# Half of each row normalisation given to GpSimd, the residual added in PSUM for three chunks only, and routing and stores reordered around it

## The chip, the core and the metric

The kernel runs on one core of one Trainium2 chip, in float32 throughout. The metric is the device time of one launch in microseconds (us). The engines named below are PE (TensorE: matmuls, with PEld for its weight loads), DVE (VectorE), ACT (ScalarE), POOL (GpSimd, which also issues the indirect DMAs) and SP (SyncE, which issues nearly all other DMAs). Each engine executes its own instructions in the order in which the program issued them, and waits on semaphores for the others.

## The reference

One transformer block with adaptive layer norm (4096 tokens of width D = 256): linear attention, and then a mixture of 8 experts of which each token uses two.

```python
def layernorm(x): return (x - mean(x)) / sqrt(var(x) + 1e-5)

sa, ca, ga, sb, cb, gb = six rows of (silu(c) @ wmod)          # ga, gb kept off zero by 0.25
h = layernorm(x) * (1 + ca) + sa
x = x + ga * attention(h)                                      # 16 heads of 64, linear attention
h = layernorm(x) * (1 + cb) + sb
p = softmax(h @ Wg + bg); top 2 of 8 experts, weights renormalised
expert_e(h) = gelu(h @ W1[e] + b1[e]) @ W2[e] + b2[e]          # 256 -> 1024 -> 256
x = x + gb * sum over the two chosen experts of weight * expert_e(h)
```

## The kernel before, in words

**Attention (0 to about 344 us).** The 4096 tokens lie in 8 chunks `xs[0..7]` of 512 tokens (128 partitions x 4 tiles x 256). `hT[i]` is the first norm's output of chunk i, transposed. All of the linear attention folds into one 256 x 256 matrix; with 8 more columns for the experts' logits it is `weff`. `raw` holds what x itself gives to the logits.

**Residual and routing (about 344 to 415 us).** `products(i)` makes chunk i of the new x and its logits: `residual(i, half, cols)` takes, for each of 4 tiles of 128 tokens, the product `hT[i]` x `weff` (two blocks of K) and then adds `xs[i]` and `raw` in the same PSUM bank by multiplying with the identity matrix. A PSUM buffer `po` holds half a chunk; there are three. `park(i)` has ACT copy both halves to `xs[i]` and `logits` (`keep`) and has SP store `xs[i]` to the output (`store`).

A `Route` then ranks the tokens of its chunks: chunks 0, 1 and 2 alone, 3 and 4 together (`r34`), and 5, 6, 7 together (`last`). Its steps, in the order in which the data needs them:

- DVE: `chunk_stats` (mean and variance of each tile), `variance`; ACT: `root` (a square root, with a table load before and after it); DVE: `finish`, `distances` (logits less their maximum), `choose` (two largest, tile `both`).
- PE: `places`, matmuls of `both` with triangular and all-one matrices into PSUM tile `pp`: each token's running number within its expert. It includes `seen`, the count of all chunks before, so that the routes are a chain.
- DVE: `weigh` (weights into `row`), `aim` (reads `pp`, makes `dest` and the new `seen`).
- ACT: `rows`, the second norm of x, tile by tile, into `row`; POOL: `begin_rows` (token numbers into `row`) and `send`: for each tile two indirect DMAs that scatter the rows to `routed` in DRAM, sorted by expert.

After three chunks `early_table` counts how many full blocks of 256 rows the experts have and fills `where` for the first 5 blocks (`EARLY`), which hold rows of chunks 0 to 2 (`FIRST`) alone. `late_table` does it for the rest.

**Expert blocks (about 415 us to the end).** `run` takes the blocks one after the other: SP loads a block's weights (`load_weights`) and rows (`load_rows`, tile `xg`), three blocks ahead; `prepare` transposes the rows (PSUM tile `ptb`, copied by ACT to `xT`); `hidden` is 32 matmul instructions into `ph` and 8 gelus on ACT (`gl`); `project` is 32 or so into `py`; `add_to_out` adds the result to the output by indirect DMAs on POOL. `steps` hangs the remaining routing of chunks 5 to 7 between the first two blocks: `places` of `last` stands on PE behind block 0's `hidden` and block 1's `prepare`, and in front of block 1's `hidden`.

**Order.** From the residual part on, every call goes through `InOrder`, so the program text is the order of each engine's queue. In the loop over chunks 0 to 2 the text is: statistics and norm of chunk i, `park(i + 1)`, `rows`, `choose`, `places`, then `products(i + 2)`, `weigh`, `aim`, `send`. Behind the loop come `early_table`, the routing of `r34` up to `power`, `products` and `park` of 5, 6 and 7 with the `rows` of `r34`, and then `load_rows(0)` and the ranks of `r34`. On SP `load_rows(0)` stands behind the stores of all eight chunks.

Of the kernel before, what the change touches and what calls it, by code (L numbers as in the profile page):

```python
# [14 lines left out]
AF = mybir.ActivationFunctionType  # L15
ALU = mybir.AluOpType
# [6 lines left out]
TPC = 4  # L23
# [25 lines left out]
def adaln_block_kernel(  # L49
# [18 lines left out]
    on = SimpleNamespace(pe=nc.tensor, dve=dve, act=nc.scalar, pool=nc.gpsimd, sp=nc.sync)  # L68
    _, N, D = x.shape
    INNER = HEADS * DH  # L70
    E, _, H = w1.shape
    KB = D // P
# [3 lines left out]
    NCH = N // CH  # L76
# [9 lines left out]
    FIRST = 3  # L86
# [22 lines left out]
    ident = const.tile([P, P], FP, tag="ident", name="ident")  # L109
# [8 lines left out]
    xs = [const.tile([P, TPC, D], FP, tag=f"x{i}", name=f"x{i}") for i in range(NCH)]  # L118
    hT = [const.tile([P, KB, CH], FP, tag=f"hT{i}", name=f"hT{i}") for i in range(NCH)]
    mv = const.tile([P, NT, 2], FP, tag="mv", name="mv")  # L120
    rstd = const.tile([P, NT], FP, tag="rstd", name="rstd")
# [8 lines left out]
    raw = const.tile([P, NT, E], FP, tag="raw", name="raw")  # L130
# [62 lines left out]
    with tc.tile_pool(name="attn", bufs=1) as attn, tc.tile_pool(  # L193
# [58 lines left out]
        for half in range(2):  # L252
            cols = slice(half * 512, (half + 1) * 512)
# [32 lines left out]
        with tc.tile_pool(name="ps_t", bufs=4, space=bass.MemoryType.PSUM) as ps_t:  # L286
# [141 lines left out]
            for i in range(NCH):  # L428
                if i + 1 < NCH:
                    xn = first_norm(i + 1)  # L430
                for t in range(TPC):
                    n = i * TPC + t
# [42 lines left out]
        with tc.tile_pool(name="ps_c", bufs=1, space=bass.MemoryType.PSUM) as ps_c:  # L475
# [10 lines left out]
            for acc in pctx:  # L486
                nc.tensor.matmul(
                    acc, zeros[:, 0, :], zeros[:, :, :HW].to_broadcast([1, PPB, HW]),
                    start=True, stop=False,
# [69 lines left out]
            for s in range(NT + LAG):  # L559
# [6 lines left out]
                if s >= LAG:  # L566
                    add_context(s - LAG)
                    after_context(s - LAG)
                    i, rest = divmod(order[s - LAG], 3)
# [6 lines left out]
            for g, pairs in enumerate(groups):  # L576
                nq, q0 = len(pairs), pairs[0]
                nc.vector.reciprocal(zr[:, q0 : q0 + nq, :], pctx[g][:, :nq, DH:HW])
                for hh in range(2):
                    r = slice(hh * DH, (hh + 1) * DH)  # L580
# [17 lines left out]
            for kb in range(KB):  # L598
                pw = ps_w.tile([P, D], FP, tag="w", name="pw")
                for q in range(PAIRS):  # L600
# [4 lines left out]
                        start=(q == 0),  # L605
                        stop=(q == PAIRS - 1),
# [33 lines left out]
    logits = table.tile([P, NT, E], FP, tag="logits", name="logits")  # L640

    def residual(i: int, half: int, cols: int):

        po = ps_r.tile([P, 2, 512], FP, tag="r", name="po")
        for z in range(2):
            t = 2 * half + z
            for kb in range(KB):
                on.pe.matmul(
                    po[:, z, :cols],
                    hT[i][:, kb, t * P : (t + 1) * P],  # L650
                    weff[:, kb, :cols],
                    start=(kb == 0),
                    stop=False,
                )
            on.pe.matmul(po[:, z, :D], ident, xs[i][:, t, :], start=False, stop=(cols == D))
            if cols > D:
                on.pe.matmul(
                    po[:, z, D:cols], ident, raw[:, i * TPC + t, :], start=False, stop=True
                )
        return po  # L660

    def attention_logits():
# [34 lines left out]
    def stats_of(n: int, src):  # L697
        st = small.tile([P, 6], FP, tag="st", name="st")
        on.dve.bn_stats(st, src)
        on.dve.bn_aggr(mv[:, n, :], st)  # L700

    def chunk_stats(i: int):
        for t in range(TPC):
            stats_of(i * TPC + t, xs[i][:, t, :])

    def keep(i: int, half: int, po, more: bool = True):

        on.act.activation(xs[i][:, 2 * half : 2 * half + 2, :], po[:, :, :D], AF.Identity)
        if more:
            n = i * TPC + 2 * half  # L710
            on.act.activation(logits[:, n : n + 2, :], po[:, :, D : D + E], AF.Identity)
# [3 lines left out]
    def products(i: int):  # L715
        parts[i] = [residual(i, half, D + E) for half in range(2)]

    def park(i: int):
        for half, po in enumerate(parts.pop(i)):
            keep(i, half, po)  # L720
        store(i)

    class Norm:

# [42 lines left out]
    shift = table.tile([P, NT], FP, tag="shift", name="shift")  # L767

    def store(i: int):
        on.sp.dma_start(ov[i], xs[i])  # L770
# [6 lines left out]
    class Route:  # L777
# [28 lines left out]

        def rows(self, c: int = 0):

            for t in range(TPC):
                n = self.n0 + c * TPC + t  # L810
                on.act.activation(
                    self.row[c][:, t, :D], xs[self.chunks[c]][:, t, :], AF.Identity,
                    bias=shift[:, n : n + 1], scale=rstd[:, n : n + 1],
                )

        def distances(self, src=None):
# [78 lines left out]
            on.dve.tensor_reduce(here, self.both.rearrange("p t e -> p e t"), AX.X, ALU.add)  # L895
            on.dve.tensor_tensor(seen[:, 0, :], seen[:, 0, :], here, ALU.add)

        def send(self, *which):

            for t in [c * TPC + t for c in which for t in range(TPC)]:  # L900
                for k in range(2):
                    ins = on.pool.indirect_dma_start(
                        lists[(self.n0 + t) * 2 + k],
                        IndirectOffsetOnAxis(ap=self.dest[:, k, t : t + 1], axis=0),
                        self.row[t // TPC][:, t % TPC, :],
                        None,
                    )
                    if self.chunks[0] >= FIRST:
                        apart(ins, later_sends, early_loads)
# [117 lines left out]
    def tiles_of(b: int):  # L1027
        return BT if b < EARLY + PAIRED else 1
# [7 lines left out]
    def load_rows(b: int):  # L1036
        nt = tiles_of(b)
        first = register(0, b, E * N - nt * P)
        xg = xpool.tile([P, BT, ROW], FP, tag="xg", name="xg")
        ins = on.sp.dma_start(  # L1040
            xg[:, :nt, :], routed[ds(first, nt * P), :].rearrange("(j p) w -> p j w", p=P)
        )
        if b < EARLY:
            apart(ins, early_loads, later_sends)
        return xg
# [137 lines left out]
    def table_for(func):  # L1183

        on.act.activation(spare[:, 1:], spare[:, :1], func)
# [8 lines left out]
    for half in range(2):  # L1194
        po = residual(0, half, D)
# [2 lines left out]
        for z in range(2):  # L1198
            stats_of(2 * half + z, po[:, z, :D])
        keep(0, half, po, more=False)  # L1200
    store(0)
    pl = first_logits()
    products(1)
    for i, (r, norm) in enumerate(zip(routes[:FIRST], norms)):
        if i > 0:
            chunk_stats(i)
        norm.variance()
        norm.root()
        table_for(AF.Exp)
        norm.finish()  # L1210
        r.distances(pl if i == 0 else None)
        r.begin_rows()
        r.power()
        park(i + 1)
        r.rows()
        r.choose()
        r.places()
        products(i + 2)
        r.weigh()
        r.aim()  # L1220
        r.send(0)
    early_table()
    r34, norm = routes[3], norms[3]
    park(4)
    chunk_stats(3)
    products(5)
    chunk_stats(4)
    norm.variance()
    norm.root()
    table_for(AF.Exp)  # L1230
    norm.finish()
    r34.distances()
    r34.begin_rows()
    r34.power()
    weights = load_weights(0, None)
    for i in range(5, NCH):
        park(i)
        if i + 1 < NCH:
            products(i + 1)
        if i > 5:  # L1240
            r34.rows(i - 6)
    loads = {0: (load_rows(0), *weights[1:])}
    r34.choose()
    r34.places()
    r34.weigh()
    r34.aim()
    r34.send(0, 1)
    last = routes[4]
    for i in last.chunks:
        chunk_stats(i)  # L1250
    norms[4].iterate()
    last.distances()
    last.choose()
    residual_psum.close()
# [4 lines left out]

    steps = {  # L1260
        (0, 1): [last.power, last.begin_rows, lambda: last.rows(0), lambda: last.rows(1), last.places],
        (0, 2): [last.weigh, last.aim, lambda: last.send(0, 1)],
        (1, 1): [lambda: last.rows(2), lambda: last.send(2)],
        (1, 2): [late_table],
    }

    pairs, order_of = list(range(EARLY + PAIRED)), []
# [88 lines left out]
```

## Time and profile before

| | |
|---|---|
| median of 8 runs | 926.48 us (923.61 to 930.95) |
| profiled execution | 926.64 us; span of its instructions 924.9 us; mean granted PE clock 0.972 |
| busy in the span | PE 880.5, DVE 370.1, ACT 349.4, POOL 356.9 us |
| residual and routing | from 344.5 us (first `po`) to 415.1 us (first `ph`) |
| block 1's `hidden` starts | 428.96 us |
| first and last scatter of rows by POOL | 362.35 and 463.14 us |

In the lines of the profile a line number is that of the kernel; L36 is the helper of `InOrder`, through which most calls go, so the tiles' names tell the instructions apart. A float32 matmul appears as two instructions. "[3.03 <-PE pp L36]" means that the engine sat idle for 3.03 us before the instruction, and that what ended the wait was PE's write of `pp`. PEclk is the clock granted to PE, 1.00 being full speed.

### The profile page before, as it was taken

How to read it: one execution, taken by the hardware profiler on the slowest of the kernel's cores; microseconds unless marked ns; L12 is line 12 of the kernel's file. 1: busy time of each engine (PE TensorE's matmuls, PEld its weight loads, DVE VectorE, ACT ScalarE, POOL GpSimd, SP SyncE). 2: the span in 40 equal slices, each digit the busy share in tenths (PEclk: the TensorE clock that was granted, in tenths of full speed). 3: DMA queues.
4: the chain of work that ended last, by engine and by line, in shares of the span. 5: the costliest groups of instructions: out<-in, count | busy, mean ns of one | idle time of the engine just before them, and what ended most of it. 6: DMA issues, size and time to landing. Idle time of an engine off the chain costs nothing. (4 is left out here: it accounts for less than half of the span.)

```text
span 924.9 us, 13061 instructions
## 1 busy us (share of the span) xinstructions
PE 880.5 (95%) x4706; PEld 665.2 (72%) x4706; DVE 370.1 (40%) x915; ACT 349.4 (38%) x642; POOL 356.9 (39%) x311
## 2 busy tenths in 40 slices
PE   7979999999999889979999999999999999999993
PEld 4544444455545578868888888888989889898883
DVE  5454453798888846545611212112112111111111
ACT  4313443344434425347233233332443333334230
POOL 2000000377998912717733333233223233232423
PEclk9978999999999979989999999999999999999997
DMA  9999950133000002469887787775897777766511
GB/s 328 354 344 351 351 168 1 45 115 114 3 1 1 1 1 95 159 215 383 296 263 191 205 261 223 229 243 178 286 346 222 243 238 247 246 214 209 153 29 30
DMA packets 124535, 175.25 MB, mean 189 GB/s; under 512 B 12428, under 2 KB 105266, under 8 KB 124468
## 3 DMA queue, kind: packets, MB, share of 16 engines
q1 hardware_dynamic: 113040, 152.78, 50.2%
q0 software_dynamic: 11424, 21.61, 8.9%
q8 instruction: 38, 0.62, 0.3%
q14 instruction: 29, 0.24, 0.1%
q10 hardware_dynamic: 4, 0.00, 0.0%
HBM read 117.69 MB, written 57.71 MB: 190 GB/s over the span
## 5 line engine op out<-in xcount | busy, mean ns | idle before, releaser
L1107 ACT ACTIVATE gl<-ph,b_sb 128x256 f32<-128x256 f32 (+1 forms) x280 | 122.2, 437 | 258.8 <-PE ph L1100 252.2
L1118 PE MATMUL py<-w_sb,gl 128*128 128x256 f32 x960 | 212.7, 379 | 0.0
L1100 PE MATMUL ph<-xT,w_sb 128*128 128x256 f32 (+1 forms) x1120 | 208.0, 344 | 1.3 <-ACT xT L1074 1.3
L1100 PEld LDWEIGHTS ph<-xT,w_sb 128*128 128x128 f32 x1120 | 184.5, 191 | 21.4 <-ACT xT L1074 2.0
L1118 PEld LDWEIGHTS py<-w_sb,gl 128*128 128x128 f32 x960 | 180.0, 190 | 23.1
L1126 DVE SCALAR_TENSOR_TENSOR y<-py,gs,gb_bc 128x256 f32<-128x256 f32 x60 | 29.0, 484 | 310.5 <-PE py L1118 306.7
L277 PE MATMUL pq<-wq,hT 128*128 128x512 f32 x256 | 118.3, 604 | 1.2 <-DVE qs L36 1.2
L277 PE MATMUL pk<-wk,hT 128*128 128x512 f32 x256 | 117.0, 610 | 0.3 <-ACT hT L178 0.3
L36 POOL DMA_INDIRECT hT<-out_dram,who x35 | 36.9, 1055 | 158.5 <-DMA out_dram<-hT,who 149.7
L277 PEld LDWEIGHTS pk<-wk,hT 128*128 128x128 f32 x256 | 48.5, 195 | 60.6 <-issue 55.6
L36 POOL DMA_INDIRECT routed<-row,dest_i x64 | 62.6, 978 | 56.1 <-ACT row L36 19.5
L277 PEld LDWEIGHTS pq<-wq,hT 128*128 128x128 f32 x256 | 46.0, 190 | 49.5 <-issue 45.9
L36 POOL DMA_INDIRECT out_dram<-y,who x33 | 52.4, 1587 | 54.3 <-DVE y L1127 25.1
L36 POOL TENSOR_TENSOR qs<-qs,qsum 128x1024 f32<-128x1024 f32 x30 | 58.1, 1937 | 15.6 <-DVE qsum L36 15.6
L36 DVE TENSOR_TENSOR qs<-qs,pk 128x1024 f32<-128x1024 f32 x31 | 37.8, 1221 | 63.5 <-ACT ka L438 45.3
L36 POOL TENSOR_TENSOR hT<-hT,y 128x256 f32<-128x256 f32 x35 | 25.2, 720 | 79.6 <-DMA hT<-out_dram,who 54.4
L36 ACT ACTIVATE qs<-qs 128x1024 f32<-128x1024 f32 x32 | 33.8, 1055 | 38.2 <-DVE qs L36 38.2
L438 ACT ACTIVATE ka<-pk 128x1024 f32<-128x1024 f32 x24 | 24.6, 1023 | 57.6 <-PE pk L277 57.6
L483 POOL MEMSET qs<- 128x8 f32 x8 | 0.8, 116 | 113.5 <-PE pt L175 82.3
L36 DVE TENSOR_REDUCE qmax<-pq 128x16 f32<-128x1024 f32 x32 | 38.6, 1206 | 13.9 <-PE pq L277 13.8
L36 POOL TENSOR_TENSOR ka<-ka,nk_bc 128x1024 f32<-128x1024 f32 x18 | 42.5, 2359 | 0.0
L539 PEld LDWEIGHTS pctx<-qs,ka 128*64 128x64 f32 x768 | 26.0, 145 | 20.7 <-issue 12.6
(256 smaller groups left out, 1006.6 us busy)
## 6 DMA issues: line engine op xcount, KB each, us to landing
w_sb<-in_L_ffn_W_dram SPq DMA_DIRECT2D x80, 1024.0 KB, 6.0
routed<-pad SPq DMA_DIRECT2D x32, 1088.0 KB, 12.9
x<-in_L_attn_x_dram SPq DMA_DIRECT2D x16, 512.0 KB, 3.9
xg<-routed SPq DMA_DIRECT2D x28, 272.0 KB, 4.6
b_sb<-b_d SPq DMA_DIRECT2D x40, 128.0 KB, 5.4
out_dram<-x SPq DMA_DIRECT2D x8, 512.0 KB, 2.7
xg<-routed SPq DMA_DIRECT2D x12, 136.0 KB, 4.4
ka<-in_L_wmod_dram SPq DMA_DIRECT2D x3, 512.0 KB, 11.8
```

Source lines behind the costliest of these rows:

```text
L36: ins = getattr(self.engine, name)(*args, **kwargs)
L277: nc.tensor.matmul(pw[:, half * 512 : (half + 1) * 512], hT[i][:, kb, t * P : (t + 1) * P], w[:, kb, half * 512 : (half + 1) * 512], start ...
L438: nc.scalar.activation(k_tile(n), pk, AF.Identity)
L483: nc.gpsimd.memset(qs[:, :, (h + 1) * HW - 1 : (h + 1) * HW], 1.0)
L539: nc.tensor.matmul(pctx[g][h * DH : (h + 1) * DH, j, :], ek[:, q * P + h * DH : q * P + (h + 1) * DH], qs[:, q, h * HW : (h + 1) * HW], st ...
L1100: on.pe.matmul(ph[:, :rows], w1_sb[:, kb, hb * P : (hb + 1) * P], xT[:, kb, :rows], start=(kb == 0), stop=(kb == KB - 1),)
L1107: on.act.activation(gl[:, hb, :rows], ph[:, :rows], AF.Gelu_apprx_tanh, bias=b1_sb[:, hb : hb + 1])
L1118: on.pe.matmul(py, gl[:, hb, j * P : (j + 1) * P], w2_sb[:, hb, :], start=(hb == 0), stop=(hb == HB - 1),)
L1126: on.dve.scalar_tensor_tensor(y, py, gs[:, j : j + 1], gb_bc, ALU.mult, ALU.mult)
```

## The change

1. For chunks 3 to 7 `residual` no longer adds `xs[i]` and `raw` in PSUM. `keep` copies the product to `hT[i]` (`parked`), and DVE adds it to `xs[i]` (`add`, one instruction over 128 x 1024, followed by the chunk's statistics) and `raw` to the logits (`add_logits`).
2. `rows` on ACT does two of a chunk's four tiles; POOL does the other two (`other_rows`) ahead of the chunk's sends. `send` takes one chunk.
3. In the loop over chunks 0 to 2, `products(2)` and `products(3)` stand before `places`; `products(4)` stands behind `early_table`. The ranks and sends of `r34` stand before `products(6)`, no longer behind `products(7)`.
4. The stores: 0 to 2 behind their chunk's sends; 3 and 4 in block 2's step, 5 to 7 in block 3's. On SP `load_rows(0)` then stands behind the stores of chunks 0 to 2 alone.

```diff
     def residual(i: int, half: int, cols: int):
         po = ps_r.tile([P, 2, 512], FP, tag="r", name="po")
+        whole = i < FIRST
         for z in range(2):
             t = 2 * half + z
             for kb in range(KB):
...
-                    stop=False,
-                )
-            on.pe.matmul(po[:, z, :D], ident, xs[i][:, t, :], start=False, stop=(cols == D))
-            if cols > D:
-                on.pe.matmul(
-                    po[:, z, D:cols], ident, raw[:, i * TPC + t, :], start=False, stop=True
-                )
+                    stop=(kb == KB - 1 and not whole),
+                )
+            if whole:
+                on.pe.matmul(po[:, z, :D], ident, xs[i][:, t, :], start=False, stop=(cols == D))
+                if cols > D:
+                    on.pe.matmul(
+                        po[:, z, D:cols], ident, raw[:, i * TPC + t, :], start=False, stop=True
+                    )
         return po
+    def parked(i: int):
+        return xs[i] if i < FIRST else hT[i].rearrange("p kb (z d) -> p (kb z) d", d=D)
     def keep(i: int, half: int, po, more: bool = True):
-        on.act.activation(xs[i][:, 2 * half : 2 * half + 2, :], po[:, :, :D], AF.Identity)
+        on.act.activation(parked(i)[:, 2 * half : 2 * half + 2, :], po[:, :, :D], AF.Identity)
...
     def park(i: int):
         for half, po in enumerate(parts.pop(i)):
             keep(i, half, po)
-        store(i)
+
+    def add(i: int):
+        on.dve.tensor_tensor(xs[i], xs[i], parked(i), ALU.add)
+        chunk_stats(i)
+
+    def add_logits(*chunks):
+        tiles = slice(chunks[0] * TPC, (chunks[-1] + 1) * TPC)
+        on.dve.tensor_tensor(logits[:, tiles, :], logits[:, tiles, :], raw[:, tiles, :], ALU.add)
         def rows(self, c: int = 0):
-            for t in range(TPC):
+            for t in range(TPC // 2):
...
+        def other_rows(self, c: int):
+            for t in range(TPC // 2, TPC):
+                n = self.n0 + c * TPC + t
+                on.pool.tensor_scalar(
+                    self.row[c][:, t, :D], xs[self.chunks[c]][:, t, :],
+                    rstd[:, n : n + 1], shift[:, n : n + 1], ALU.mult, ALU.add,
+                )
-        def send(self, *which):
-            for t in [c * TPC + t for c in which for t in range(TPC)]:
+        def send(self, c: int = 0):
+            self.other_rows(c)
+            for t in range(c * TPC, (c + 1) * TPC):
...
         r.rows()
         r.choose()
+        if i + 1 < FIRST:
+            products(i + 2)
         r.places()
-        products(i + 2)
         r.weigh()
         r.aim()
-        r.send(0)
+        r.send()
+        store(i)
     early_table()
     r34, norm = routes[3], norms[3]
+    products(4)
     park(4)
-    chunk_stats(3)
-    products(5)
-    chunk_stats(4)
+    add(3)
+    add(4)
...
     norm.finish()
+    add_logits(*r34.chunks)
     r34.distances()
     r34.begin_rows()
     r34.power()
     weights = load_weights(0, None)
-    for i in range(5, NCH):
-        park(i)
-        if i + 1 < NCH:
-            products(i + 1)
-        if i > 5:
-            r34.rows(i - 6)
-    loads = {0: (load_rows(0), *weights[1:])}
+    products(5)
+    park(5)
+    r34.rows(0)
+    r34.rows(1)
     r34.choose()
     r34.places()
     r34.weigh()
     r34.aim()
-    r34.send(0, 1)
+    r34.send(0)
+    r34.send(1)
+    for i in (6, 7):
+        products(i)
+        park(i)
+    loads = {0: (load_rows(0), *weights[1:])}
     last = routes[4]
     for i in last.chunks:
-        chunk_stats(i)
+        add(i)
     norms[4].iterate()
+    add_logits(*last.chunks)
     last.distances()
     last.choose()
...
-        (0, 2): [last.weigh, last.aim, lambda: last.send(0, 1)],
+        (0, 2): [last.weigh, last.aim, lambda: last.send(0), lambda: last.send(1)],
...
+        (2, 2): [lambda: store(3), lambda: store(4)],
+        (3, 2): [lambda: store(5), lambda: store(6), lambda: store(7)],
```

More of the change, by code (lines that the diff above doesn't have):

```diff
@@ L904, in send @@
                         IndirectOffsetOnAxis(ap=self.dest[:, k, t : t + 1], axis=0),
-                        self.row[t // TPC][:, t % TPC, :],
+                        self.row[c][:, t % TPC, :],
                         None,
@@ L1200, in adaln_block_kernel @@
         keep(0, half, po, more=False)
-    store(0)
     pl = first_logits()
```

## The prediction

> **What bounds the kernel now.** I read the page first, then windows of the stretch that the change touches, then its timeline instruction by instruction.
>
> ```profile
> PE 880.5 (95%) x4706; PEld 665.2 (72%) x4706; DVE 370.1 (40%) x915; ACT 349.4 (38%) x642; POOL 356.9 (39%) x311
> ...
> PE   7979999999999889979999999999999999999993
> ...
> PEclk9978999999999979989999999999999999999997
> ```
>
> PE is busy 95% of the span. The few digits below 9 in slices 14 to 18 (the residual part) come with a lower granted clock. The windows say how such time counts:
>
> ```profile
> 353.20:377.40 24.20, 22.27 (x129) 19.92 (x128) 17.70 (x92) 16.38 (x37) 11.72 (x13) 1.00 0.36 133
> 377.40:397.80 20.40, 17.51 (x85) 15.14 (x84) 11.53 (x56) 5.68 (x14) 12.55 (x16) 0.92 0.57 196
> ...
> 410.70:415.10 4.40, 1.33 (x6) 0.82 (x5) 3.76 (x16) 1.45 (x4) 1.96 (x2) 0.71 0.86 251
> ...
> 429.00:464.00 35.00, 35.00 (x170) 30.80 (x169) 17.75 (x71) 17.31 (x37) 26.91 (x31) 1.00 0.86 317
> ```
>
> The first column behind the length is PE: from 429 us on, when block 1's `hidden` starts, PE never pauses (35.00 of 35.00). So whatever moves the start of that `hidden` (428.96 us) moves the end by the same amount. Ahead of it PE has pauses, and they cost twice, as PE alone in windows of 3.41 us shows:
>
> ```profile
> 374.94:378.35 3.41, 2.48 (x18) 1.00 0.58 217
> 378.35:381.76 3.41, 3.41 (x11) 0.51 0.39 141
> ...
> 395.41:398.82 3.41, 1.05 (x5) 1.00 1.03 383
> 398.82:402.24 3.42, 3.42 (x11) 0.52 0.91 341
> ...
> 409.06:412.48 3.42, 1.89 (x17) 1.00 0.55 182
> 412.48:415.89 3.41, 1.86 (x6) 0.51 0.87 247
> 415.89:419.30 3.41, 3.41 (x10) 0.50 0.91 298
> ```
>
> After a window with a pause, or filled with the small matmuls of `places`, the whole next window has half the clock (0.51), until a window has been full. Last, who waits:
>
> ```profile
> 360.74 0.22 DVE L36 TENSOR_TENSOR of_hot<-hots,pp 128x64 f32<-128x64 f32 x1 [3.03 <-PE pp L36]
> ...
> 376.25 0.30 PEld L36 LDWEIGHTS pp<-both,before 128*128 128x128 f32 x2 [1.02 <-DVE both L36]
> ...
> 385.65 0.17 DVE L36 TENSOR_TENSOR cnt<-pcnt,region 128x8 f32<-128x8 f32 x1 [6.92 <-PE pcnt L36]
> ...
> 410.98 0.29 DVE L36 TENSOR_TENSOR of_hot<-hots,pp 128x128 f32<-128x128 f32 x1 [10.15 <-PE pp L36]
> ...
> 413.75 1.09 PE L36 MATMUL ptb<-ident,xg 128*128 128x128 f32 x4 [2.81 <-DVE st L36]
> ...
> 426.01 0.43 PE L36 MATMUL pp<-both,before 128*128 128x96 f32 x2 [1.19 <-DVE both L36]
> ```
>
> Two chains are about equally long. DVE's (`aim`, statistics, `choose`) takes 8.4 us a chunk (`of_hot` at 360.74, 369.20, 377.59), and PE waits for `both` 1.0 us each time. PE's products fill the rest, so that in the end DVE waits 6.9 and 10.2 us for PE. Then PE waits 2.8 us at 413.75, in truth for the rows `xg`, issued on SP at 410.69 behind the last store.
>
> **PE's matmuls.** In the timeline a tile of `residual` takes 1.54 us (353.24 to 354.78), of which x takes 0.43 and `raw` 0.14; residual(0), 256 columns wide, has 0.86 for the rest. Between 0.89 and 0.97 I take 0.92: 0.62 x 20 tiles = 12.4 us less PE work. That is a gain only where PE ends last.
>
> **The order around `places`.** In the first chunk `both` is ready at 356.5, but products(2), 4 x 1.54 = 6.2 us, now stands in front: `of_hot` comes at 366.9, not 360.74. DVE's queue is in order: behind `aim` wait the statistics of chunk 1 and all its routing. `both` of chunk 1 then ends 7.07 us later as before (360.74 to 367.81), at 374.0. PE meanwhile does half of products(3) by 368.5 and stops, since its second half needs the PSUM buffer that `keep` of chunk 2 frees at 372.7 (5.8 us behind `of_hot`, as at 366.5 before). That pause halves the clock: the second half takes 2.9 us, `places` 1.1, `of_hot` 376.8. Chunk 2: `both` at 383.8; PE has had nothing for 7 us, `places` takes 2.2 us for 1.1, `of_hot` 386.2. That is 8.6 us behind 377.59.
>
> **The table and chunks 3 and 4.** The count for `early_table` stood behind products(4) on PE (the 6.92 us). Now it goes first, and the table ends at 393.0, against 390.8. Then come two adds. The nearest rows: 1.22 us for a DVE product of two SBUF tensors of that size (at 328.37, POOL idle), and 2.48 beside a POOL elementwise (321.13). POOL is mostly sending here, and beside sends the 128x240 operations of `late_table` take 0.40 us, as short as their elements allow; so I take 1.3 with the gap (range to 2.5). 2 x 1.3, statistics 4.3, `add_logits` 0.25 (row of a 128x64 `far`), and the same 4.35 us to `both`: 404.5, against 399.43.
>
> **PE behind it.** products(4) and (5), 7.4 us of work partly at half clock, run from 387.7 to 397.2. `places` of r34 now stands ahead of products(6): PE idles 7.3 us to 404.5. At half clock `places` takes 4.1 us for 2.05, and of 7.4 us of products(6) and (7) some 3.7 us of time run at half, so 9.2: they end at 417.9. Before, they ended at 408.9.
>
> **Block 0.** `keep` writes `hT[i]`, which the second half of the products still reads, so both copies of chunk 7 follow 417.9, and end at 419.3 (two of 0.60, two of 0.18, overlapped). The transposes and `xT` lead to `ph` at 420.3 (before 415.1). It runs at full clock, 7.1 us for the 9.3 of before: end at 427.4 (424.4).
>
> **Block 1.** DVE: add(7) at 419.3, 1.3; statistics 2.1; `iterate` 3.2; logits and `distances` 1.4; `choose` 2.7: `both` at 430.0 (425.87). PE has waited 2.2 us; `places` of `last` takes 2.95 us, or 5.8 at half clock. `hidden` starts at 433.0 or 435.9: 4.0 or 6.9 us late. The pause is like that ahead of 398.82, where the clock fell, so I take 6.9.
>
> The Trainium skill, "TensorE: Matmul & The Clock Gate", Part 1, has the clock fall after an idle window of about 3.4 us and rise after one busy window; here windows that were 1.05, 1.89 and even 2.48 us busy were enough. By that rule the gap of 2.2 us costs nothing and the 7.3 us one only 1.7, and the sum would be an estimated +1.7 us; the rows go against it, and I keep them.
>
> **POOL and ACT.** Two row tiles a chunk go from ACT (4 took 2.06 us) to POOL. ACT's 1.0 us is worth nothing: it waits for DVE's `rstd` next. On POOL no row shows a tensor_scalar; the nearest are 0.72 us (two inputs, 128x256) and 0.32 (affine_select, 128x128). I take 0.45, nearer to the one-input row; both ends stay. The eight sends of a chunk take 8 x 1.275 = 10.2 us and now start at 367.5; with two pauses of 1.2 to 1.6 us the early sends end at 401 (before 393.2). The rows of block 0 need some 2.4 us to land and 3 to be read back: 406.5, with 12 us to spare before 418.7. SP no longer waits for the last store with it, but PE isn't there yet. The last sends end at about 470 (464.1) and block 5, which needs them, is transposed at about 485: POOL's tensor_scalar would have to take 2 us to matter.
>
> The Trainium skill, "GPSIMD Engine Reference", section 4.1, sends elementwise work to VectorE and calls GpSimd's one-input operations roughly line-rate, an estimated 0.2 us plus dispatch here; by it the sum stays as it is.
>
> **SP.** Five stores (512 KB, median 2.7 us to land) leave a stretch with idle DMA for 447 to 470 us, behind the loads of blocks 4 and 5. SP sits blocked there today, from 454 to 466, until the rows of block 5 can be read. The loads run two blocks (28 us) ahead, which hides 3 x 0.6 us of issue and some 7 us of transfer; without that cover, up to 3 us.
>
> **Sum.** 428.96 + 6.9 = 435.9 at `hidden` of block 1, and all behind it moved alike: 926.48 + 6.9 = 933.4 us (the profiled execution, 926.64, is within 0.2 us of the median). A difference under 0.5% (4.6 us) can't be told from none in this kernel.
>
> **The rivals.** (A) The clock doesn't fall at the smaller pauses: 4.0 us or less late, and with no falls at all in the changed kernel, where the kernel before loses 5.6 us to them, 924: from 924 to 931. For it: the window from 422.72 was only 2.23 us busy and the clock held; where the windows fall differs between executions. (B) The adds run at 2.5 us beside `other_rows`: on the path lie those of chunks 3, 4 and 7, 3 x 1.2, and the longer pauses may cost another window, 1.7: 937 to 940. Against it: POOL elementwise is on for only 1 us in 11. (C) Not slower: PE, not DVE, ends last. The 12.4 us of matmuls would then count. The place is the wait of PE at `places` of r34: it would have to come at 397.2, straight behind products(5). Then products(7) ends at 406.6, `ph` begins at 409, `both` of `last` comes 12.1 us behind products(7), at 418.7, and `hidden` at 421.7: 919 us. It decides once the chain of DVE is 7 us shorter than worked out; against it stand the 8.4 us per chunk measured, with 6.2 us of products put into it.
>
> **How the numbers follow.** Forecast 0.55 (931.5 to 937), A 0.20 (924 to 931), B 0.13, C 0.12. Slower by over 0.5% (above 931.1): the forecast, B and 0.02 of A, 0.70. Within: 0.18 of A and 0.03 of C, 0.21. Faster: 0.09. The range, 925 to 939.5, leaves out about 0.11 below and 0.07 above.
>
> **What would show it.** In the changed profile: `of_hot` of chunk 2 near 386, PE idle some 7 us ahead of `places` of r34, half clock in `places` and products(6), `both` of `last` near 430, `hidden` of block 1 near 436, no wait for `xg` at block 0, PE full from there on. Wrong if `places` of r34 finds PE busy, if the clock stays at 1.00 over those pauses, or if PE pauses behind 440 us for rows or weights.

## The result, and the profile after

The changed kernel takes 935.28 us (median of 11 runs; one of them, at 963.85 us, ran disturbed and is left out of the ratio). The kernel before has a median of 925.60 us over the 32 runs beside it. The ratio is 1.0103, with a 95% interval of 1.0079 to 1.0127: 9.5 us slower (7.3 to 11.8), where 6.9 was forecast. The profiled execution took 932.42 us.

Three lines of the page of the changed kernel: PE's row of the table, PE's busy tenths and its clock, in 40 slices.

```profile
PE 872.8 (94%) x4626; PEld 658.2 (71%) x4626; DVE 379.8 (41%) x922; ACT 342.0 (37%) x626; POOL 370.0 (40%) x327
...
PE   7979999999999898668999999999999999999994
...
PEclk9979999999999998577999999999999999999998
```

PE is busy 7.7 us less than before (880.5), and the span is 5.7 us longer. The hole in both rows now lies in slices 16 to 19; before, PE's row had it in slices 14, 15 and 18 and the clock's in 15 and 18. The windows of the changed kernel by stage (behind the length: PE, PEld, DVE, ACT, POOL busy, PE's clock, DMA share, GB/s):

```profile
374.80:395.20 20.40, 12.16 (x42) 10.30 (x43) 16.14 (x73) 6.42 (x15) 16.22 (x19) 0.59 0.30 97
395.20:418.80 23.60, 15.07 (x58) 12.22 (x56) 16.95 (x58) 8.10 (x22) 12.79 (x14) 0.71 0.89 304
418.80:434.70 15.90, 13.20 (x62) 12.00 (x63) 11.04 (x50) 11.11 (x19) 12.28 (x17) 0.82 0.89 303
434.70:470.00 35.30, 35.30 (x160) 30.77 (x160) 18.29 (x68) 12.29 (x26) 26.04 (x29) 0.94 0.72 243
```

From 374.8 to 418.8 PE is busy 27 of 44 us at 0.59 to 0.71 of its clock, and DVE 33 of 44. From block 1's `hidden` (434.7) on, PE is full again. Who waits for whom, from the timeline of the changed kernel, PE and DVE:

```profile
362.58 0.22 DVE L36 TENSOR_TENSOR of_hot<-hots,pp 128x64 f32<-128x64 f32 x1 [9.17 <-PE pp L36]
...
368.39 3.88 PE L36 MATMUL po<-weff,hT 128*128 128x264 f32 x8 [3.99 <-ACT logits L36]
...
372.07 0.47 PE L36 MATMUL pp<-both,before 128*128 128x32 f32 x2
...
374.29 0.22 DVE L36 TENSOR_TENSOR of_hot<-hots,pp 128x64 f32<-128x64 f32 x1 [3.54 <-PE pp L36]
...
381.72 0.61 PE L36 MATMUL pp<-both,before 128*128 128x32 f32 x2 [7.47 <-DVE total L36]
...
384.07 0.22 DVE L36 TENSOR_TENSOR of_hot<-hots,pp 128x64 f32<-128x64 f32 x1 [1.32 <-PE pp L36]
...
391.14 1.22 DVE L36 TENSOR_TENSOR x<-x,hT 128x1024 f32<-128x1024 f32 x1
...
403.11 0.69 PE L36 MATMUL pp<-both,before 128*128 128x64 f32 x2 [7.17 <-DVE both L36]
...
417.67 0.66 PE L36 MATMUL ptb<-ident,xg 128*128 128x128 f32 x4 [0.88 <-ACT logits L36]
...
429.14 0.71 PE L36 MATMUL pp<-both,before 128*128 128x96 f32 x2 [2.70 <-DVE g L36]
...
434.76 9.31 PE L36 MATMUL ph<-xT,w_sb 128*128 128x256 f32 x32
```

DVE waits 9.17 us for `pp` of chunk 0, behind the products that now stand ahead of `places`. From there on it is PE that waits for DVE: 7.47 us before `places` of chunk 2, 7.17 before those of r34, 2.70 before those of `last`. Small instructions of DVE that run beside one of POOL's pairs of row tiles take longer. Here is such a place in the changed kernel, ahead of `places` of r34:

```profile
399.31 0.42 DVE L36 TENSOR_TENSOR far<-far,gate_c 128x64 f32<-128x64 f32 x1
...
399.48 1.19 POOL L36 TENSOR_SCALAR row<-x,rstd,shift 128x256 f32<-128x256 f32 x2
...
400.28 0.46 DVE L36 SCALAR_TENSOR_TENSOR hots<-far,rank 128x64 f32<-128x64 f32 x1
```

and here the same two in the kernel before, where POOL has no row tiles:

```profile
396.11 0.22 DVE L36 TENSOR_TENSOR far<-far,gate_c 128x64 f32<-128x64 f32 x1
...
396.88 0.23 DVE L36 SCALAR_TENSOR_TENSOR hots<-far,rank 128x64 f32<-128x64 f32 x1
```

Last, the clock, in PE's windows of 3.41 us:

```profile
364.19:367.60 3.41, 0.21 (x1) 0.99 0.25 82
367.60:371.02 3.42, 2.63 (x6) 0.50 0.50 194
371.02:374.43 3.41, 3.23 (x13) 0.50 0.45 163
...
394.91:398.32 3.41, 1.03 (x5) 0.99 1.01 355
398.32:401.73 3.41, 0.00 (x0) 0.50 1.06 379
401.73:405.15 3.42, 2.04 (x10) 0.50 0.36 116
...
415.39:418.80 3.41, 2.05 (x11) 1.00 1.02 405
418.80:422.21 3.41, 3.40 (x16) 1.00 1.08 391
...
425.62:429.04 3.42, 0.82 (x6) 0.99 0.72 172
429.04:432.45 3.41, 3.31 (x16) 0.50 0.97 356
432.45:435.86 3.41, 3.41 (x15) 0.50 1.07 388
435.86:439.28 3.42, 3.42 (x10) 0.51 0.33 114
```

The windows that are 0.21, 1.03 and 0.82 us busy are each followed by half clock (0.50), and it lasts through all of `places`: the window from 371.02 is 3.23 us busy, mostly with its small matmuls, and the next ones stay at 0.50. The window of 2.05 us at 415.39 is followed by 1.00. The Trainium skill ("TensorE: Matmul & The Clock Gate", Part 1) asks for an idle window before the clock falls; here windows that were a quarter busy were enough, as in the kernel before.

The two profiled executions entered the residual part at different times: the first `po` starts at 344.57 us before and at 340.23 after, though nothing ahead of it was changed (in all profiles of this case it lies between 340.2 and 346.8; in these two, half clock covered more of 320 to 340 us before than after). So the table counts from the first `po`.

| us behind the first `po` | before | predicted after | measured after |
|---|---|---|---|
| `of_hot` of chunk 0 | 16.17 | 22.3 | 22.35 |
| `of_hot` of chunk 1 | 24.63 | 32.2 | 34.06 |
| `of_hot` of chunk 2 | 33.02 | 41.6 | 43.84 |
| `places` of r34 starts | 64.18 | 59.9 | 62.88 |
| products(7) ends | 64.3 | 73.3 | 76.55 |
| `ph` of block 0 | 70.54 | 75.7 | 78.58 |
| `places` of `last` starts | 81.44 | 85.4 | 88.91 |
| `hidden` of block 1 starts | 84.39 | 91.3 | 94.53 |

### The profile page after: what moved, and what is told of

It is laid out like the page before. It is cut to its first block, busy times and chain, and to the rows that moved or that the text cites. A ratio compares the mean times of both kernels' runs of the same rounds, so it can differ in the third digit from the quotient of the medians.

```text
span 930.6 us, 12903 instructions
## 1 busy us (share of the span) xinstructions
PE 872.8 (94%) x4626; PEld 658.2 (71%) x4626; DVE 379.8 (41%) x922; ACT 342.0 (37%) x626; POOL 370.0 (40%) x327
## 5 line engine op out<-in xcount | busy, mean ns | idle before, releaser
L36 POOL DMA_INDIRECT routed<-row,dest_i x64 | 66.7, 1042 | 43.8 <-issue 15.7
L36 POOL DMA_INDIRECT out_dram<-y,who x33 | 52.5, 1591 | 57.3 <-DVE y L1149 25.2
L36 POOL TENSOR_TENSOR hT<-hT,y 128x256 f32<-128x256 f32 x35 | 25.2, 721 | 76.3 <-DMA hT<-out_dram,who 51.4
L438 ACT ACTIVATE ka<-pk 128x1024 f32<-128x1024 f32 x24 | 24.6, 1024 | 56.9 <-PE pk L277 56.9
L36 DVE TENSOR_REDUCE qmax<-pq 128x16 f32<-128x1024 f32 x32 | 38.6, 1206 | 13.9 <-PE pq L277 13.8
L36 PE MATMUL po<-weff,hT 128*128 128x264 f32 (+1 forms) x128 | 39.1, 459 | 4.0 <-ACT logits L36 4.0
```

The costliest lines, as they stand in the source:

```text
L36: ins = getattr(self.engine, name)(*args, **kwargs)
L438: nc.scalar.activation(k_tile(n), pk, AF.Identity)
```

## The experiments

Twelve runs were made on three other chips, named A, B and C here. On all three the kernel before itself takes longer than in the first measurement: medians of 966.47 (A), 971.33 (B) and 967.17 us (C), not 925.60. So each ratio is to the kernel before on the same chip. The second column counts from that profile's first `po`; the third is PE's longest idle time between `hidden` of block 1 and 500 us.

| kernel | chip | median us, ratio (95%) | `hidden` of block 1 | longest idle of PE |
|---|---|---|---|---|
| before (first measurement) | | 925.60 | 84.39 | none over 0.7 |
| changed (first measurement) | | 935.28, 1.0103 (1.0079 to 1.0127) | 94.53 | none over 0.7 |
| b_again: before | B | 970.88 (one run) | 101.65 | 17.69 |
| a_again: changed | B | 953.03, 0.9789 (0.9743 to 0.9836) | 93.92 | 2.83 |
| a_third: changed | C | 950.70, 0.9839 (0.9808 to 0.9870) | 94.49 | 3.49 |
| e1_places_first | A | 945.59, 0.9786 (0.9751 to 0.9822) | 87.80 | 5.53 |
| e1_again | C | 946.07, 0.9787 (0.9755 to 0.9818) | 90.26 | 3.23 |
| e2_x_in_psum | B | 964.44, 0.9942 (0.9905 to 0.9978) | 104.38 | 5.04 |
| e3_act_rows | A | 962.23, 0.9947 (0.9925 to 0.9970) | 95.65 | 19.52 |
| e4_r34_late | C | 947.77, 0.9815 (0.9783 to 0.9848) | 95.87 | 3.75 |
| e5_before_swapped | A | 976.96, 1.0134 (1.0096 to 1.0172) | 112.57 | 17.49 |
| e6_filled | A | 953.93, 0.9859 (0.9826 to 0.9893) | 93.95 | 2.96 |
| e7_first_and_psum | B | 960.10, 0.9837 (0.9778 to 0.9897) | 102.62 | 7.64 |
| e9_pool_rows_alone | C | 940.76, 0.9755 (0.9717 to 0.9794) | 90.34 | 3.84 |

The table has two stories. Up to `hidden` of block 1 the changed kernel runs as in the first measurement (94.53, 93.92, 94.49). The kernel before doesn't: 101.65 instead of 84.39, and then it stands still twice more. On chips B and C the change is therefore 1.6 to 2.1% faster. The first experiments test the schedule; the last ones the standstill.

**e1_places_first and e1_again: `places` ahead of products(2) and (3) again**, the rest of the change left in.

```diff
-        if i + 1 < FIRST:
-            products(i + 2)
         r.places()
+        if i + 1 < FIRST:
+            products(i + 2)
```

> The changed kernel with one part undone: in the loop over chunks 0 to 2 places stands ahead of products(2) and products(3) again. Theory (products(2) ahead of the first places sets the chain of DVE back by 6.2 us, and PE's pauses halve its clock): the 6.2 us and one or two windows of half clock come back, so about 2 us faster than the kernel before (from 5 faster to 2 slower), aim of chunk 2 some 33 us behind the first po, as before. Rival 'adds' (the five adds on DVE cost the time): still 6 to 9 us slower than before. Rival 'POOL' (its share of the rows costs the time): still 9 us slower.

> The changed kernel with places ahead of products(2) and products(3), as in the kernel before. Theory (the order around places holds DVE's chain up): hidden of block 1 comes 5 to 9 us earlier behind the first po than in the changed kernel of the same call, and the time is lower by as much, 0.991 to 0.995 of it. Against the kernel before: 0.995 to 1.000 on a chip where PE makes no unexplained pauses beside the sends, 0.975 to 0.985 where it does. Rival (the adds or POOL's share are what costs time): within 0.3% of the changed kernel.

`hidden` of block 1 came 6.1 us earlier than in a_again (on another chip) and, on chip C, where both ran, 4.2 us earlier than in a_third (90.26 against 94.49), just short of the 5 to 9 expected. The medians there are 946.07 and 950.70, a quotient of 0.995: 4.6 us, about the step seen at `hidden`. The part of the forecast that put a loss at this order stands. But `aim` of chunk 2, expected some 33 us behind the first `po`, came at 36.5 (e1) and 39.6 (e1_again), with DVE waits of 2 to 3.2 us that the profile puts down to "remote". The forecast against the kernel before missed on chip A, since it knew nothing of these chips. And e1_again is still 5.3 us above e9 on the same chip, which has nothing of the change but the rows: the order accounts for about half of the 9.9 us between a_third and e9, and no run assigns the rest.

**e5_before_swapped: the same order put alone into the kernel before.**

```diff
         r.choose()
+        if i + 1 < FIRST:
+            products(i + 2)
         r.places()
-        products(i + 2)
+        if i + 1 == FIRST:
+            products(i + 2)
```

> The kernel before with one part of the change: products(2) and products(3) ahead of places in the loop, all else as before. Theory: the chain is set back by 6.2 us and two pauses as in the changed kernel, and here products(4) to (7) with x in PSUM still follow, 24.6 us of PE work, so 8 to 15 us slower than before, about 12. Rival 'adds' and rival 'POOL': as fast as before, within 2 us, since PE only does the same matmuls in another order.

1.34% slower (9 to 17 us), and `hidden` of block 1 10.9 us behind that of b_again (on another chip). `of_hot` of chunk 0 comes at 22.36 us behind the first `po`, as in the changed kernel (22.35) and as predicted (22.3). The order around `places` is enough by itself to cost as much as the whole change cost in the first measurement.

**e2_x_in_psum and e7_first_and_psum: x and `raw` added in PSUM for all chunks**, by the matmuls with the identity; e7 has `places` first as well.

```diff
-        whole = i < FIRST
+        whole = True
...
-        return xs[i] if i < FIRST else hT[i].rearrange("p kb (z d) -> p (kb z) d", d=D)
+        return xs[i]
...
-        on.dve.tensor_tensor(xs[i], xs[i], parked(i), ALU.add)
...
-    add_logits(*r34.chunks)
...
-    add_logits(*last.chunks)
```

> The changed kernel with x and raw added in PSUM for all eight chunks, so without the adds on DVE. Theory: both of chunks 3 and 4 comes 2.9 us earlier, but products(6) and (7) behind it are 4.9 us longer; hidden of block 1 starts within 2 us of the changed kernel, some 10 us behind the kernel before. Rival 'adds' (the five adds on DVE cost the time): back to within 3 us of the kernel before.

> The changed kernel with places ahead of products(2) and (3) again and x in PSUM for all chunks; what is left is POOL's share of the rows, the ranks of chunks 3 and 4 ahead of products(6), and the stores further down. Theory: the chain starts as in the kernel before, and the rows of block 0 no longer wait for the last store, so hidden of block 1 starts 80 to 84 us behind the first po and the whole is 0 to 7 us faster than before, about 4. Rival 'POOL': still some 9 us slower than before.

Against a_again on the same chip e2 loses 11.4 us (964.44 against 953.03), with `hidden` of block 1 10.5 us later: products(7) ends 8.8 us later behind the first `po` (85.94 against 77.19). Of these 8.8, 5.0 lie in products(6) and (7), which take 13.8 us instead of 8.84 with the matmuls that DVE's adds replace. The other 3.8 lie ahead of `places` of r34: DVE waits 5.17 us there for ACT's copy of chunk 4, behind the longer products(4). So the adds on DVE do not cost; taken with the matmuls that they replace they gain in this order, and the expectation of e2, 2.9 us earlier at `both` of chunks 3 and 4 and `hidden` within 2 us, missed. In e7 `hidden` of block 1 came at 102.62 where 80 to 84 was expected, 12 to 15 us later than in the two e1 runs, with a pause of 5.66 us at block 0 that no wait explains among it; e2 has one of 5.54 us at the same place. The hope that the two edits together would beat e1 fell.

**e4_r34_late: ranks and sends of r34 behind products(6), (7) and `load_rows(0)`.**

```diff
     r34.rows(1)
+    for i in (6, 7):
+        products(i)
+        park(i)
+    loads = {0: (load_rows(0), *weights[1:])}
     r34.choose()
...
     r34.send(1)
-    for i in (6, 7):
-        products(i)
-        park(i)
-    loads = {0: (load_rows(0), *weights[1:])}
```

> The changed kernel with the ranks and sends of r34 behind products(6), products(7) and load_rows(0), as in the kernel before. Theory (DVE's chain sets the end, and PE's 7 us pause ahead of places of r34 costs little because products(6) and (7) are not what is late): hidden of block 1 0.5 to 2 us later than in the changed kernel of the same call, last po 5 to 7 us earlier, time 1.000 to 1.003 of the changed kernel's. Rival (the pause ahead of places of r34 and the half clock behind it is what costs): 3 to 6 us faster than the changed kernel, 0.993 to 0.997.

The times in the profile follow the theory: products(7) ends 8.3 us earlier (68.26 us behind the first `po`, against 76.51; 5 to 7 were expected) and `hidden` of block 1 1.4 us later than in a_third (95.87), since PE then waits 9.30 us for `both` of `last` instead of 2.70. The medians differ the other way, 947.77 against 950.70, by 2.9 us, and the intervals overlap. So the sign of what the move of r34 is worth stays open.

**e6_filled: unread matmuls in PE's pauses** (8 ahead of the second half of products(3), 12 and 13 ahead of `places` of chunk 2 and r34, 3 ahead of those of `last`), to hold the clock.

```diff
+    def fill(n: int):
+        idle = psum_of("idle", D)
+        for _ in range(n):
+            on.pe.matmul(idle, ident, weff[:, 0, :D], start=True, stop=True)
...
+        if i + 1 == FIRST:
+            fill(12)
         r.places()
...
+    fill(13)
     r34.places()
```

> The changed kernel with matmuls that nobody reads in PE's pauses: 8 ahead of the second half of products(3), 12 ahead of places of chunk 2, 13 ahead of places of chunks 3 and 4, 3 ahead of places of chunks 5 to 7 (0.44 us each at full clock). No result changes. Theory: the clock stays up over most of the pauses and the set-back of the chain alone is left: 4 to 6 us less than the changed kernel, so 3 to 6 us slower than before. Without the clock's part in it (rivals 'adds' and 'POOL', or the chain alone): no faster than the changed kernel, 9 us slower than before or more.

`hidden` of block 1 did not move (93.95). Ahead of `places` of chunk 2 and of r34 the matmuls ended before the pause did: 4.99 and 2.47 us of idle time were left, and the windows behind them were at 0.50 as before. At chunk 1 they held the clock, which is 1.00 in the windows from 372 to 381 us of this profile:

```profile
376.48 2.05 PE L36 MATMUL po<-weff,hT 128*128 128x264 f32 x8 [0.54 <-ACT prob L36]
...
379.18 0.39 PE L36 MATMUL pp<-seen,ones 128*128 128x32 f32 x2
...
382.26 0.22 DVE L36 TENSOR_TENSOR of_hot<-hots,pp 128x64 f32<-128x64 f32 x1 [3.42 <-remote]
```

The second half of products(3) took 2.05 us instead of 3.88, and `places` was done at 379.57. But DVE went on only at 382.26, held by something that the profile calls "remote": 11.60 us behind `of_hot` of chunk 0, as in a_third (11.71). So nothing was gained there on this chip, and no run here shows what the half clock alone costs; it is read from the rows of the first measurement, where `of_hot` started within 0.1 us of the end of `places`.

**e3_act_rows: all four row tiles on ACT again**, none on POOL.

```diff
-            for t in range(TPC // 2):
+            for t in range(TPC):
...
-            self.other_rows(c)
```

> The changed kernel with all four row tiles of a chunk on ACT again, none on POOL. Theory: POOL's tensor_scalars lie beside its waits or ahead of blocks that need the rows much later, so as slow as the changed kernel, 9 us slower than before, within 1.5 us. Rival 'adds': the same 9 us. Rival 'POOL': back to within 2 us of before.

`hidden` of block 1 comes 1.1 to 1.7 us later than in the changed kernel (three profiles). That would agree with POOL's and ACT's shares being worth little there, but this profile has pauses on the way that the others lack, among them 5.24 us of PE ahead of the second half of products(4), so it settles little. The time was expected within 1.5 us of the changed kernel's, and that missed: the ratio of 0.9947 stands over 1% above those of the changed kernel on chips B and C. Behind `hidden` it stands still. The windows of e3, and PE's line from its timeline:

```profile
455.00:465.00 10.00, 0.76 (x4) 0.33 (x2) 0.00 (x0) 0.00 (x0) 7.56 (x9) 0.74 0.29 105
465.00:475.00 10.00, 0.00 (x0) 0.00 (x0) 0.97 (x2) 0.00 (x0) 7.86 (x7) 0.50 0.52 163
```

```profile
475.28 2.08 PE L36 MATMUL ph<-xT,w_sb 128*128 128x256 f32 x4 [19.52 <-issue]
```

For 20 us PE, DVE and ACT do next to nothing; only POOL works, at its sends. "issue" says that the profile has no wait for it.

**b_again: the kernel before once more**, with a profile.

> The kernel before, profiled beside the next three on their chip, because the first four runs were on a chip where it takes 966 us. Both theories: the same instructions; if the time is again near 966 us its extra 40 us must show as pauses behind 430 us, where the first profile has none.

The same standstill, of 17.69 us here. In the first measurement PE was busy 10.00 of 10.00 in every window of 10 us between 430 and 500. Here, by the windows of b_again and then by its timeline:

```profile
470.00:480.00 10.00, 0.38 (x1) 0.00 (x0) 0.00 (x0) 0.00 (x0) 7.56 (x9) 0.62 0.29 104
480.00:490.00 10.00, 0.58 (x1) 0.50 (x2) 1.56 (x6) 1.57 (x4) 4.63 (x5) 0.50 0.29 70
```

```profile
442.46 0.71 PE L36 MATMUL pp<-both,before 128*128 128x96 f32 x2 [8.42 <-issue]
...
461.42 0.69 SPq L36 DMA_DIRECT2D xg<-routed  x1
...
480.94 0.97 POOL L36 DMA_INDIRECT routed<-row,dest_i  x1 [0.31 <-issue]
482.22 0.97 POOL L36 DMA_INDIRECT routed<-row,dest_i  x1 [0.30 <-issue]
483.50 1.61 POOL L36 DMA_INDIRECT out_dram<-y,who  x1 [0.30 <-issue]
...
488.28 0.37 SPq L36 DMA_DIRECT2D w_sb<-in_L_ffn_W_dram  x1
...
488.28 0.48 DVE L36 SCALAR_TENSOR_TENSOR y<-py,gs,gb_bc 128x256 f32<-128x256 f32 x1 [18.74 <-remote]
...
488.41 1.57 ACT L36 ACTIVATE gl<-ph,b_sb 128x256 f32<-128x256 f32 x4 [27.79 <-remote]
...
489.42 2.93 PE L36 MATMUL ph<-xT,w_sb 128*128 128x256 f32 x6 [17.69 <-DVE cnt L36]
```

POOL issues 24 sends without a break, one every 1.28 us, from 452.83 to 483.19. SP issues nothing between 462 and 488. SP, DVE, ACT and PE all go on within 1.2 us of each other, 5 us behind the last of them. The pause of 8.42 us ends with the last of a run of 16 sends, which runs from 441.64 to 442.61.

**a_again and a_third: the changed kernel**, for comparison on chips B and C.

> The changed kernel, for the comparison on one chip. Theory (chain set back by 6.2 us, clock halved in PE's pauses): hidden of block 1 starts 94 to 95 us behind the first po, 10 us later than in the kernel before; the whole is slower by that, unless pauses behind block 1 differ. Rivals: the same 10 us, since they speak of its cause.

> The changed kernel itself, as the measure for the other three. Theory (schedule alone): hidden of block 1 about 10 us later behind the first po than in the first profile of the kernel before, ratio 1.007 to 1.013 on a chip where the engines make no unexplained pauses beside the sends; 0.975 to 0.983 where they do. Rival (the sign of the change hangs on the execution, not on the chip): the ratio lies between the two.

Faster than before on both chips, by 2.1% and 1.6% (a_third's ratio lies just outside the 0.975 to 0.983 expected), so the sign goes with the chip (or with what else differs between the measurements), not with the execution. The 10 us that a_again was expected to be behind the kernel before at `hidden` did not come, as the kernel before was itself late there (101.65). PE's pauses are there too, but short: 1.41, 1.10, 1.74, 1.03 and 3.49 us in a_third between 455 and 480.

**e9_pool_rows_alone: the kernel before with nothing changed but the rows.** POOL does two of a chunk's four tiles, ahead of that chunk's eight sends.

```diff
-            for t in range(TPC):
+            for t in range(TPC // 2):
...
             for t in [c * TPC + t for c in which for t in range(TPC)]:
+                if t % TPC == 0:
+                    self.other_rows(t // TPC)
```

> The kernel before with nothing changed but the rows: two of a chunk's four tiles on POOL ahead of the chunk's sends. Theory (ACT's share is worth nothing, DVE and PE set the end): 0.998 to 1.002, hidden of block 1 within 1 us of the kernel before. Rival (a run of sends without a break holds the other engines up, and POOL's row tiles break it): where the engines pause beside the sends, 0.985 to 0.992, and the longest pause of PE is under 10 us instead of 17.7.

The fastest kernel of all on that chip: 940.76 us, 2.45% below the kernel before (2.1 to 2.8%). The theory that ACT's and POOL's shares are worth nothing fell on this chip, and the rival was too modest. Its windows and its timeline:

```profile
440.00:450.00 10.00, 10.00 (x51) 8.84 (x50) 0.97 (x2) 2.72 (x6) 7.96 (x10) 1.00 0.69 231
450.00:460.00 10.00, 8.75 (x41) 6.91 (x40) 8.41 (x34) 1.90 (x4) 7.83 (x10) 1.00 0.66 224
460.00:470.00 10.00, 5.52 (x14) 3.76 (x14) 4.82 (x18) 3.03 (x6) 7.70 (x9) 0.66 0.57 195
```

```profile
447.91 1.09 POOL L36 TENSOR_SCALAR row<-x,rstd,shift 128x256 f32<-128x256 f32 x2
...
459.31 1.20 POOL L36 TENSOR_SCALAR row<-x,rstd,shift 128x256 f32<-128x256 f32 x2
...
465.92 5.73 PE L36 MATMUL py<-w_sb,gl 128*128 128x256 f32 x16 [3.84 <-issue]
```

The 24 sends are the same, but two pairs of row tiles now cut them into three runs of eight, with some 2.3 us from send to send there instead of 1.28. PE's longest pause is 3.84 us, where b_again, on chip B, has 17.69 (on chip C the kernel before left no profile). Nor is this the only pair: on chip A e3, without these tiles, has 19.52 us, and e6 and e1, with them, 2.96 and 5.53. So with POOL's row tiles there is no long standstill, without them one. That it is the break which does it, and not ACT's lighter share, is not shown: e3 and e9 move the two together. And e9 does not take away every pause: DVE still stands for 6.14 us ("remote") at `of_hot` of chunk 2.

Set beside a_third on the same chip, the rest of the change costs 0.9839 / 0.9755 = 1.009: 0.9%, about what the whole change cost in the first measurement (1.03%), where there was no standstill to break.

## Why the prediction was right, and where its sizes were off

**The bound and the direction.** "Whatever moves the start of that `hidden` moves the end by the same amount" held: the output rows of every block from 440 to 919 us (DVE's `y`) come 8.0 us later in the changed profile, with no drift. Of these 8.0, the later start of `hidden` behind the first `po` makes 10.14, the slower run of `hidden` itself 2.2, and the earlier first `po` takes off 4.34. The spans differ by only 5.7, as the last read of the output for POOL's add waited 4.16 us before and 2.23 after, which is a matter of the execution. The chain alone, 10.14 and 2.2, would give 12.3; the medians, over executions that start and end differently, give 9.7. The interval of 7.3 to 11.8 does not reach down to the 6.9 of the sum.

**The order around `places`.** Chunk 0 was right to 0.1 us. Chunk 1 is the first term that was mis-sized: the sum took 2.9 us for the second half of products(3), which has only about 1.1 of half clock in it (two tiles at the sum's 0.92 us are 1.84), and 1.1 for `places`, with none. The pause there was 3.99 us, the half clock lasted over both, and up to the end of `places` they took 3.7 (368.39 to 372.07) and 2.2 us (to 374.25). That is the 1.9 us between 32.2 and 34.06, and everything behind it inherits it. The order itself is shown by experiment: e5 adds it alone and e1 takes it away. The price of the half clock is read from these rows, and e6 did not confirm it.

The other misses in the table have a cause that the sum put at nothing: what POOL's row tiles do to DVE. Rival B had only the adds slowed beside POOL, and "POOL's tensor_scalar would have to take 2 us to matter" counts POOL's own queue alone. But one or two of DVE's small instructions beside each pair of them take about twice as long: `far` and `hots` ahead of `places` of r34 0.42 and 0.46 us instead of 0.22, the first step of the table 0.47 instead of 0.20, a step of the statistics of `last` 0.45 instead of 0.17. The profiles of a_again and a_third show the same; before, where ACT does all the rows, and e3 do not. All of these lie in DVE's chain. They make up most of what it missed, which was 0.4 us at chunk 2, 0.7 at `places` of r34 and 0.5 at those of `last`. What `hidden` gains without them no run shows by itself, since e3 has other pauses.

**Adds, statistics, table.** The adds took 1.19 to 1.23 us each, against 1.3 with the gap: right. Rival B (2.5 us beside POOL) was not put to the test: none of the five adds lay beside a pair of POOL's row tiles. e2 shows that the adds, taken with the matmuls they replace, are a gain of 11 us in this order, on its chip. The sum held that in its products of 0.92 us a tile, and put no name to it.

**PE behind it.** Predicted: 7.3 us idle ahead of `places` of r34, 4.1 us for them at half clock. Measured: 7.17 and, from 403.11 to 407.00, 3.9. products(6) and (7) took 9.78 us (9.2). Rival C, PE last at this place, did not come up; rival A neither: the clock fell at each of these pauses.

**Blocks 0 and 1.** The rows were there in time: SP issued `xg` at 403.42, 14 us ahead of the transposes, and `ptb` waited for `logits`, not for `xg`. `places` of `last` found 2.70 us of idle time (2.2 predicted) and took 5.6 us at half clock (5.8). One loss was not in the sum: the half clock lasts to 439.28, into `hidden` of block 1, whose 32 matmuls took 9.31 us instead of 7.10. In total the forecast missed 3.2 us ahead of `hidden` and 2.2 in it.

**POOL and ACT.** The pairs of row tiles took 1.08 to 1.19 us, 0.54 to 0.60 each, where 0.45 was taken between 0.32 and 0.72. The Trainium skill ("GPSIMD Engine Reference", section 4.1) gave an estimated 0.2 us plus dispatch; the measured 0.54 to 0.60, dispatch included, is more than double 0.2. In the first measurement the pairs showed in DVE's small instructions, as said; from block 1's `hidden` on PE was full where the sends ran. Whether "ACT's 1.0 us is worth nothing" is right for the schedule e3 leaves open, with its `hidden` 1.1 to 1.7 us later and pauses of its own. That the step could do something quite different, and end a long standstill, no row of the trace of before suggested; on chip C it is worth 2.45%.

**SP.** The late stores cost nothing that shows: PE is full from 440 to 490.

## What to carry to other kernels

When two engines have chains of nearly equal length, follow both queues past a reordering: moving 6.2 us of matmuls ahead of the small ones that the next chunk waits for delayed both chains, and the pauses came back as half clock. Price a pause of a TensorE queue with the window behind it and with whatever runs until a window of large matmuls has been full, small matmuls and the next stage included; by the rows, that was some 4 of the 5.4 us that the sum missed behind the first `po`. Most of the rest lies, again by the rows, in small instructions of DVE that took twice as long beside work given to POOL, an engine off the path; so look at what the other engines do at that moment, too. And a ratio from one chip may not carry over: look at whether the kernel before behaves the same, and try each part of a change alone, since here, on one chip, one part was worth 2.45% and the rest cost 0.9%.

## What the hardware showed that was not expected

On chips A and B, in the kernels whose ACT does all the rows (e3, e5, b_again), PE, ACT, DVE and SP stood still together, for 17.5 to 19.5 us of PE, while POOL issued indirect DMAs back to back, and went on 4 to 6 us behind the last send. Shorter pauses came on all three chips, in the kernels with rows on POOL too; some ended in the middle of a run of sends (e2, e7). In the first measurement the same program, with the same sends every 1.27 to 1.35 us, had PE full throughout. By the profile of b_again the kernel before loses 17.3 of the 44.3 us of its longer span between the first `po` and `hidden` of block 1, and 25.2 behind it; pauses of this kind account for most of it. What holds the engines up is not settled: the profile names no wait ("issue", "remote"), and the DMA engines are at a share of only 0.29 to 0.52 in the standstills of b_again and e3. Whether e9's kernel is also the better one where there is no standstill was not tried.

And small DVE instructions took about twice their time beside POOL's tensor_scalar of 128x256: 0.38 to 0.47 us against 0.17 to 0.23, at all four pairs of row tiles between 374 and 422 us of the changed kernel.
